# Respreading the start of a fused cross-attention and factor-sum kernel: row statistics and bias on VectorE, the second group's attention beside ten products

## The chip, the cores and the metric

The kernel runs on one core of a Trainium2 chip. That core has five engines, each of which works through its own instruction queue in order: TensorE (PE, with its weight loads, PEld, beside it), VectorE (DVE), ScalarE (ACT), GpSimd (POOL) and SyncE (SP), which here only issues DMAs. [...]The metric is device time in microseconds (us) of one execution; lower is better.

## The reference

`x` is 8 batches of 1024 rows of 1024 float32 values; each batch has 64 memory rows with a mask, and there are eight 1024x1024 factors. Cut to what matters:

```python
def _layernorm(x, eps=1e-05):
    m = mean(x); v = var(x)
    return (x - m) / sqrt(v + eps)

def xattn(h, mem, mask):
    scores = einsum('bsd,bmd->bsm', h, mem) / sqrt(D)
    scores = where(mask, scores, -1e30)
    out = einsum('bsm,bmd->bsd', softmax(scores), mem)
    return where(any(mask), out, 0)

def ffn(h, factors, bias):
    return einsum('btd,rde->bte', h, factors) / sqrt(8) + bias

x = x + xattn(layernorm(x), ctx, mask)
x = x + ffn(layernorm(x), factors, bias)
```

The sum over `r` can be done first: with W = the sum of the eight factors, the second line is one 1024x1024 product per row. W has to be summed once, from 32 MB of factors, before the products can be finished.

## The kernel before, in words

**Tiling.** The 8192 rows are 16 groups (`NG`) of 512 rows, two groups to a batch. A group is four tiles of 128 rows, `x_g_t`, kept in a pool `xpool` of 12 buffers of 512 KB, from which the centred memory `memc` of a batch is also drawn. Another pool, `big`, has nine buffers of 1 MB: factor slices `f`, blocks `xb` of x, transposed x (`xT`), normalized rows `h`, their re-laid copy `hb` and the transposed rows `hT` all come from it. A tile whose buffer is still in use makes its first writer wait.

**Products.** The row product is done by a Winograd scheme: for each half group q (two row tiles) seven products (`UNITS`, u = 0 to 6) of 4 matmuls each, which the trace counts as 8, from left operands that `combine_rows` makes on VectorE and right operands that `combine_factors` makes from the quadrants of W. `product(g, q, u)` issues the matmuls into a PSUM bank, and `give(g, q, u)` adds the bank to the rows on VectorE. A group has 14 products.

**First part: four factor steps.** Each of four steps (`step` 0 to 3) sums two of W's eight chunks of rows. In round s = 0 to 3 of a step, SP loads two 1 MB factor slices, `f` (factor s) and `fp` (factor 4+s); TensorE adds `fp` into four PSUM banks by products with the identity (`sum_on_pe`, L423), VectorE adds `f` into SBUF (L535, from round 1 on), and then `beside(step, s)` issues a piece of attention work. At the end of a step VectorE adds the PSUM banks to the SBUF sums (L540) and combines (L429 to L433). The next step's L423 matmuls need the banks that L540 reads.

**Attention of a group.** Row statistics (`row_sums` and `row_squares` on ScalarE, then a power on GpSimd giving `rs`), transposes of x, `scores` (L205), `scores_back` (L221), `softmax` (L230 to L242; its first step needs `rs`), `weights_back` (L252 to L258), `read_out` (L268) and `residual` (L279) per half group; then `norm_stats` (VectorE, and four small GpSimd operations, L292 to L296), `normalize` (ScalarE, L308), and either `transpose_h_pe` (group 0) or `relayout` (16 DMAs of 64 KB, L327) followed by `transpose_rows` (VectorE, L334). `add_bias` adds the bias to the rows (GpSimd, L320). For a new batch, `centre_memory` (L109 to L112) makes `memc` on ScalarE with one small GpSimd step (L111), and `transpose_memory` (L120) transposes it on TensorE.

**Order.** All engines issue in the order in which the program is written, so the order of the calls in `beside` and in the loop over groups is the order in every queue. The attention of groups 0 and 1 and four products of group 0 (two of each half, `unit`) are in `beside`; the ten products of group 0 that are left are the first pass (g = 0) of the loop over groups. Passes g = 1 to 15 do 14 products each with the attention of group g+1, and the loads and transposes for g+2, beside them. In the first pass `store(0, 0)` is issued on SP at k = 7, `centre_memory(1)` at k = 9 and `transpose_memory(1)` at k = 11 (k counts 0 to 13 and includes the four products done earlier).

Of the kernel before, what the change touches and what calls it, by code (L numbers as in the profile page):

```python
# [20 lines left out]
def kernel(  # L21
# [81 lines left out]
    def centre_memory(b: int):  # L103


        m = st["mem", b]
        mc = xpool.tile([P, D], F32, tag="x", name=f"memc_{b}")
        msum = small.tile([P, 1], F32, tag="msum", name=f"msum_{b}")
        nc.scalar.activation(mc[:M], m[:M], AF.Copy, accum_out=msum[:M])  # L109
        mneg = small.tile([P, 1], F32, tag="mneg", name=f"mneg_{b}")  # L110
        nc.gpsimd.tensor_scalar_mul(mneg[:M], msum[:M], -1.0 / D)  # L111
        nc.scalar.activation(mc[:M], m[:M], AF.Identity, bias=mneg[:M])  # L112
        st["memc", b] = mc

    def transpose_memory(b: int):

        mc = st.pop(("memc", b))
        ps = bank(f"memTp_{b}")
        for c in range(NC):
            nc.tensor.transpose(ps[:, ts(c, M)], mc[:M, c::NC], ident[:M, :M])  # L120
        mT = work.tile([P, NC, M], F32, tag="memT", name=f"memT_{b}")
        nc.scalar.copy(mT.rearrange("p c m -> p (c m)"), ps)
        st["memT", b] = mT
# [19 lines left out]
    def row_sums(g: int):  # L143
        s1 = small.tile([P, 4], F32, tag="s1", name=f"sum_{g}")
        junk = work.tile([P, D], F32, tag="junk", name=f"junk_{g}")
        for t in range(4):
            nc.scalar.activation(junk, st["x", g, t], AF.Copy, accum_out=s1[:, t : t + 1])  # L147
        nmean = small.tile([P, 4], F32, tag="nmean", name=f"nmean_{g}")
        nc.gpsimd.tensor_scalar_mul(nmean, s1, -1.0 / D)  # L149
        st["nmean", g] = nmean  # L150

    def row_squares(g: int):
# [10 lines left out]
        nc.gpsimd.tensor_tensor(rs, rs, neghalf, ALU.pow)  # L163
        st["rs", g] = rs

    def transpose_blocks(g: int, h: int):
        xb = st["xb", g, h]
        xT = big_tile([P, NC, 8 * Q], f"xT_{g}_{h}")
        nc.vector.transpose(  # L169
            xT.rearrange("p c (t j) -> p t c j", j=Q), xb.rearrange("p t (i c) -> p t c i", i=Q)  # L170
        )
        st["xb", g, h] = xT
# [10 lines left out]
    def transpose_x_pe(g: int, h: int):  # L183
        xT = big_tile([P, NC, 2 * P], f"xT_{g}_{h}")
        flat = xT.rearrange("p c t -> p (c t)")
        rows = [st["x", g, 2 * h + t] for t in range(2)]
        transpose_rows_pe(rows, 2, 2, lambda c0: flat[:, c0 * 2 * P : (c0 + 2) * 2 * P])
        st["xb", g, h] = xT
# [84 lines left out]
    def residual(g: int, q: int):  # L273
        rden = st["rden", g]
        for n in range(2):
            for h in range(2):
                xt = st["x", g, 2 * h + q][:, ts(n, H)]
                k = 2 * q + h
                nc.vector.scalar_tensor_tensor(  # L279
                    xt, st.pop(("ro", g, q, n, h)), rden[:, k : k + 1], xt, ALU.mult, ALU.add  # L280
                )
# [32 lines left out]
            )  # L314
        st["h", g, q] = h2

    def add_bias(g: int, q: int):
        for h in range(2):
            xt = st["x", g, 2 * h + q]
            nc.gpsimd.tensor_add(xt, xt, bias_bc)  # L320

    def relayout(g: int, q: int, eng):
        h2 = st.pop(("h", g, q))
# [120 lines left out]
    nc.vector.tensor_reduce(valid, maskf, AX.X, ALU.max)  # L444
    nc.vector.tensor_scalar(maskf, maskf, NEG, -NEG, ALU.mult, ALU.add)

    done = set()

    def unit(g: int, q: int, u: int):
        product(g, q, u)  # L450
        give(g, q, u)
        done.add((g, q, u))

    def beside(i: int, s: int):
        if (i, s) == (0, -1):
            centre_memory(0)
            transpose_memory(0)
            transpose_x_pe(0, 0)
            transpose_x_pe(0, 1)
            scores(0)  # L460
            row_sums(0)
            row_squares(0)
        if (i, s) == (0, 0):
            scores_back(0)
        if (i, s) == (0, 1):
            softmax(0)
            nc.scalar.dma_start(bias_bc, bias.partition_broadcast(P))
        if (i, s) == (0, 2):
            weights_back(0)
            read_out(0, 0)  # L470
            residual(0, 0)
        if (i, s) == (0, 3):
            norm_stats(0, 0)
            read_out(0, 1)
            residual(0, 1)
        if (i, s) == (1, 0):
            normalize(0, 0, False)
            norm_stats(0, 1)
            transpose_h_pe(0, 0)
        if (i, s) == (1, 1):  # L480
            add_bias(0, 0)
            normalize(0, 1, False)
            transpose_h_pe(0, 1)
        if (i, s) == (1, 2):
            combine_rows(0, 0)
            load_rows(1, nc.sync)
        if (i, s) == (1, 3):
            add_bias(0, 1)
        if (i, s) == (2, 0):
            unit(0, 0, 0)  # L490
            unit(0, 0, 1)
        if (i, s) == (2, 1):
            combine_rows(0, 1, (1,))
            transpose_x_pe(1, 0)
        if (i, s) == (2, 2):
            transpose_x_pe(1, 1)
            row_sums(1)
        if (i, s) == (2, 3):
            scores(1)
            row_squares(1)  # L500
        if (i, s) == (3, 0):
            scores_back(1)
            softmax(1)
        if (i, s) == (3, 1):
            weights_back(1)
            read_out(1, 0)
            residual(1, 0)
        if (i, s) == (3, 2):
            norm_stats(1, 0)
            read_out(1, 1)  # L510
            normalize(1, 0)
            relayout(1, 0, nc.scalar)
            residual(1, 1)
        if (i, s) == (3, 3):
            norm_stats(1, 1)
            normalize(1, 1)
            relayout(1, 1, nc.scalar)
            unit(0, 1, 0)
            unit(0, 1, 1)

    for step in range(NS):
# [20 lines left out]
    ring[:] = COMMON  # L542


    for g in range(NG):
        n, m = g + 1, g + 2
        more, most = n < NG, m < NG
        attend = more and n > 1
        fresh = most and m % GPB == 0
        if g > 0:  # L550
            store(g - 1, 1, nc.sync)
        if most:
            load_blocks(m, nc.sync)
            load_rows(m, nc.sync)
        for k in range(14):
            q, u = divmod(k, 7)
            if (g, q, u) not in done:
                product(g, q, u)
            if k == 0:
                if g > 0:  # L560
                    combine_rows(g, 0, (4, 3))
                if attend:
                    scores(n)
            if k == 1:
                if g > 0:
                    transpose_rows(g, 1)
                if attend:
                    scores_back(n)
            if k == 2 and attend:
                softmax(n)  # L570
            if k == 3:
                if attend:
                    weights_back(n)
                if g > 0:
                    combine_rows(g, 1, (1, 2))
            if k == 4:
                if attend:
                    read_out(n, 0)
                if most:
                    row_sums(m)  # L580
                combine_rows(g, 1, (4, 3) if g > 0 else (2, 4, 3))
                if g > 0:
                    add_bias(g, 1)
            if k == 5 and attend:
                residual(n, 0)
            if k == 6 and attend:
                norm_stats(n, 0)
                read_out(n, 1)
            if k == 7:
                if fresh:  # L590
                    load_memory(m // GPB, nc.sync)
                store(g, 0, nc.sync)
                if attend:
                    normalize(n, 0)
                    relayout(n, 0, nc.sync)
                    residual(n, 1)
            if k == 8 and more:
                if attend:
                    norm_stats(n, 1)
                add_bias(n, 0)  # L600
                if attend:
                    normalize(n, 1)
                    relayout(n, 1, nc.sync)
            if k == 9 and most:
                transpose_blocks(m, 0)
                if fresh:
                    centre_memory(m // GPB)
                row_squares(m)
            if k == 10 and most:
                transpose_blocks(m, 1)  # L610
            if k == 11 and fresh:
                transpose_memory(m // GPB)
            if k == 12 and more:
                transpose_rows(n, 0)
            if k == 13 and more:
                combine_rows(n, 0, (1, 2))
            if (g, q, u) not in done:
                give(g, q, u)
    store(NG - 1, 1, nc.sync)


# [26 lines left out]
```

## Time and profile before

| What | Time or value |
|---|---|
| median of 3 runs | 1045.17 us (1044.82 to 1047.14) |
| the profiled execution, its own time | 1046.43 us |
| its span, first to last instruction | 1044.6 us |
| PE busy | 1000.0 us (96%) |
| DVE / ACT / POOL busy | 659.8 / 359.3 / 224.6 us |
| mean granted TensorE clock | 0.984 |
| 13.6 to 192.5 us (factor steps and ten products): PE busy, clock | 152.18 of 178.90 us, 0.90 |
| 192.5 to 1044.6 us (groups 1 to 15): PE busy, clock | 847.79 of 852.10 us, 1.00 |

How to read it: the first matmul is at 13.62 us, and the first product of group 1 starts at 192.48 us. From there to the end TensorE is almost always busy at full clock. The stretch between those two points is where the trace has idle time of TensorE and a clock below 1. A timeline line gives the start, the time from the first to the last of the merged instructions, the engine, the line of the program, the operation with output and inputs, the count, and in brackets how long the engine had been idle and who ended that.

### The profile page before, as it was taken

Reading aid. Unit: us, or ns where it says so; the run is one execution under the profiler, and the core shown is the slowest. Engines: PE = TensorE matmul, PEld = TensorE weight load, DVE = VectorE, ACT = ScalarE, POOL = GpSimd, SP = SyncE. Lnnn points to the kernel's source line nnn. Section 1 sums busy time; section 2 is a strip of 40 time slices with the busy share of each in tenths; the row PEclk is TensorE's granted clock in tenths of the full one; section 3 lists DMA queues with packets and bytes.
Section 4 is the critical chain, followed back from the end, with each engine's and each line's share of the span. In section 5 each row is a group of like instructions: output and inputs, shape, how many; then the busy total and the mean of one; then the engine's idle time right before and its main releaser. Section 6 shows DMA issues by size and latency. Waiting matters only on the chain.

```text
span 1044.6 us, 8939 instructions
## 1 busy us (share of the span) xinstructions
PE 1000.0 (96%) x2912; PEld 447.8 (43%) x2912; DVE 659.8 (63%) x875; ACT 359.3 (34%) x537; POOL 224.6 (22%) x255
## 2 busy tenths in 40 slices
PE   4789887999999999999999999999999999999998
PEld 3245333444444444444444444444444444444443
DVE  1595666476675858585766767585857676685541
ACT  4322332233442526241434335252524234340300
POOL 0150001031222213040412222130404022240400
PEclk9889899999999999999999999999999999999999
DMA  9877637636556474828474556638482746540321
GB/s 322 323 289 317 239 83 218 153 107 157 161 151 165 99 197 121 221 81 192 135 167 133 139 143 170 172 105 215 110 212 89 169 156 154 158 108 33 91 81 50
DMA packets 93519, 166.89 MB, mean 160 GB/s; under 512 B 12320, under 2 KB 71840, under 8 KB 89376
## 3 DMA queue, kind: packets, MB, share of 16 engines
q1 hardware_dynamic: 90464, 163.10, 54.0%
q10 hardware_dynamic: 3008, 3.21, 1.3%
q8 instruction: 23, 0.38, 0.2%
q14 instruction: 24, 0.20, 0.1%
HBM read 101.25 MB, written 33.55 MB: 129 GB/s over the span
## 4 chain that ended last, share of the span: by engine, by line
PE 88%; issue 4%; DVE 3%; DMA 2%; ACT 2%; POOL 1%; SPq 0%; ACTq 0%; DVEq 0%; POOLq 0%
PE yu L385 40%; PE yv L385 20%; PE yz L385 11%; PE ro L268 6%; PE scT L205 6%; PE sum L423 2%; DMA f<-in_L_ffn_factors_dram 1%; ACT junk L158 1%; DMA mem<-in_ctx_dram 1%; PE memTp L120 1%; DVE x L279 1%; PE tp L180 1%; DVE st L289 1%; DVE b L535 1%; POOL x L320 0%
## 5 line engine op out<-in xcount | busy, mean ns | idle before, releaser
L385 PE MATMUL yu<-t,hT 128*128 128x512 f32 x512 | 230.2, 592 | 0.0
L308 ACT ACTIVATE h<-x,nb,rstd 128x1024 f32<-128x1024 f32 x64 | 137.4, 2196 | 233.4 <-POOL nb L296 156.3
L398 DVE SCALAR_TENSOR_TENSOR x<-yu,x 128x512 f32<-128x512 f32 x128 | 88.0, 688 | 160.9 <-PE yu L385 160.9
L320 POOL TENSOR_TENSOR x<-x,bias_bc 128x1024 f32<-128x1024 f32 x64 | 152.3, 2402 | 0.0
L385 PEld LDWEIGHTS yu<-t,hT 128*128 128x128 f32 x512 | 96.2, 190 | 115.8 <-issue 115.8
L385 PE MATMUL yu<-t,s 128*128 128x512 f32 x256 | 116.1, 596 | 4.0 <-DVE t L432 4.0
L385 PE MATMUL yz<-b,hT 128*128 128x512 f32 x256 | 119.4, 610 | 0.0
L385 PE MATMUL yu<-b,hT 128*128 128x512 f32 x256 | 116.5, 598 | 0.0
L385 PE MATMUL yv<-t,s 128*128 128x512 f32 x256 | 116.5, 598 | 0.0
L385 PE MATMUL yv<-b,s 128*128 128x512 f32 x256 | 116.1, 596 | 0.0
L169 DVE STREAM_TRANSPOSE xT<-xb 128x2048 f32<-128x2048 f32 x28 | 109.8, 3922 | 0.0
L398 DVE SCALAR_TENSOR_TENSOR x<-yv,x 128x512 f32<-128x512 f32 x64 | 43.7, 683 | 97.9 <-PE yv L385 93.2
L149 POOL TENSOR_SCALAR nmean<-sum 128x4 f32<-128x4 f32 x16 | 4.1, 257 | 437.1 <-ACT junk L147 437.1
L279 DVE SCALAR_TENSOR_TENSOR x<-ro,rden,x 128x512 f32<-128x512 f32 x128 | 87.4, 744 | 16.7 <-PE ro L268 16.7
L289 DVE BATCH_NORM_STATS2 st<-x 128x6 f32<-128x512 f32 x128 | 80.2, 668 | 0.0
L385 PEld LDWEIGHTS yv<-b,s 128*128 128x128 f32 x256 | 49.2, 192 | 62.3 <-issue 62.3
L147 ACT ACTIVATE junk<-x 128x1024 f32<-128x1024 f32 x64 | 67.5, 1055 | 24.0 <-DMA x<-in_x_dram 21.5
L385 PEld LDWEIGHTS yu<-b,hT 128*128 128x128 f32 x256 | 47.5, 190 | 65.1 <-issue 65.1
L385 PEld LDWEIGHTS yz<-b,hT 128*128 128x128 f32 x256 | 47.7, 193 | 64.3 <-issue 52.5
L158 ACT ACTIVATE junk<-x,nmean 128x1024 f32<-128x1024 f32 x64 | 73.3, 1145 | 1.9 <-POOL nmean L149 0.4
L385 PEld LDWEIGHTS yv<-t,s 128*128 128x128 f32 x256 | 47.5, 190 | 59.9 <-issue 57.2
L385 PEld LDWEIGHTS yu<-t,s 128*128 128x128 f32 x256 | 47.5, 190 | 58.9 <-issue 54.0
(67 smaller groups left out, 796.4 us busy)
## 6 DMA issues: line engine op xcount, KB each, us to landing
x<-in_x_dram SPq DMA_DIRECT2D x64, 512.0 KB, 10.2
f<-in_L_ffn_factors_dram SPq DMA_DIRECT2D x32, 1024.0 KB, 11.1
out_dram<-x SPq DMA_DIRECT2D x64, 512.0 KB, 2.9
xb<-in_x_dram SPq DMA_DIRECT2D x112, 256.0 KB, 7.1
hb<-h SPq DMA_DIRECT2D x448, 64.0 KB, 2.0
mem<-in_ctx_dram SPq DMA_DIRECT2D x14, 256.0 KB, 3.8
hb<-h ACTq DMA_DIRECT2D x32, 64.0 KB, 2.1
mem<-in_ctx_dram ACTq DMA_DIRECT2D x2, 256.0 KB, 10.4
```

The lines of the kernel that those rows point to most:

```text
L147: nc.scalar.activation(junk, st["x", g, t], AF.Copy, accum_out=s1[:, t : t + 1])
L158: nc.scalar.activation(junk, st["x", g, t], AF.Square, bias=nmean[:, t : t + 1], accum_out=ss[:, t : t + 1])
L169: nc.vector.transpose(xT.rearrange("p c (t j) -> p t c j", j=Q), xb.rearrange("p t (i c) -> p t c i", i=Q))
L205: nc.tensor.matmul(ps[ts(h, M), : 2 * P], mT[:, c, :], st["xb", g, h][:, c, :], start=(c == 0), stop=(c == NC - 1),)
L268: nc.tensor.matmul(ps, eT[ts(h, M), q, :], m[ts(h, M), ts(n, H)], start=True, stop=True)
L279: nc.vector.scalar_tensor_tensor(xt, st.pop(("ro", g, q, n, h)), rden[:, k : k + 1], xt, ALU.mult, ALU.add)
L289: nc.vector.bn_stats(stats[:, n, :], xt[:, ts(n, H)])
L308: nc.scalar.activation(dst, src, AF.Identity, bias=nb[:, h : h + 1], scale=rstd[:, h : h + 1],)
L320: nc.gpsimd.tensor_add(xt, xt, bias_bc)
L385: nc.tensor.matmul(ps, lhs[:, c, :], wq[rhs][:, c, :], start=(first and c == 0), stop=(c == KH - 1), skip_group_check=True,)
L398: nc.vector.scalar_tensor_tensor(xt, st["y", g, q, key], ISR, xt, ALU.mult, ALU.add)
L423: nc.tensor.matmul(banks[c, n], ident, f[:, c, ts(n, H)], start=first, stop=last)
```

## The change

The change touches the order of work up to group 1, and nothing after it.

- Group 0's row statistics: `row_sums(0)` and `row_squares(0)` on ScalarE are replaced by `row_stats(0)` on VectorE (8 `bn_stats`, 4 `bn_aggr`, two GpSimd operations), issued first of all, and `transpose_x_pe(0, 0)` is put ahead of `centre_memory(0)`.
- Group 0's attention is spread over more rounds (steps 0 to 2), and its `add_bias` is done by VectorE.
- Group 1's attention up to `softmax(1)` stays in the factor steps, one piece a round; the rest (`weights_back(1)` to `transpose_rows(1, 0)`) moves beside the ten products, which get a loop of their own (k = 0 to 9). Its relayouts are issued by SP instead of ScalarE.
- In that loop `load_memory(1)` is at k = 4, `store(0, 0)` and `centre_memory(1)` at k = 6 behind `relayout(1, 1)`, `transpose_memory(1)` at k = 8 and `add_bias(1, 0)` at k = 9.
- The loop over groups starts at g = 1 with the same order as before; its conditions become shorter.

```diff
+    def row_stats(g: int):
+        mv = small.tile([P, 4, 2], F32, tag="mvx", name=f"mvx_{g}")
+        for t in range(4):
+            stats = small.tile([P, 2, 6], F32, tag="stats", name=f"stx_{g}_{t}")
+            for n in range(2):
+                nc.vector.bn_stats(stats[:, n, :], st["x", g, t][:, ts(n, H)])
+            nc.vector.bn_aggr(mv[:, t, :], stats)
+        rs = small.tile([P, 4], F32, tag="rs", name=f"rs_{g}")
+        nc.gpsimd.tensor_scalar(rs, mv[:, :, 1], EPS, float(D), ALU.add, ALU.mult)
+        nc.gpsimd.tensor_tensor(rs, rs, neghalf, ALU.pow)
+        st["rs", g] = rs
...
-    def add_bias(g: int, q: int):
+    def add_bias(g: int, q: int, eng=nc.gpsimd):
...
-            nc.gpsimd.tensor_add(xt, xt, bias_bc)
+            eng.tensor_add(xt, xt, bias_bc)
...
         if (i, s) == (0, -1):
+            row_stats(0)
+            transpose_x_pe(0, 0)
             centre_memory(0)
+            transpose_x_pe(0, 1)
             transpose_memory(0)
-            transpose_x_pe(0, 0)
-            transpose_x_pe(0, 1)
             scores(0)
-            row_sums(0)
-            row_squares(0)
...
         if (i, s) == (0, 2):
             weights_back(0)
+        if (i, s) == (0, 3):
             read_out(0, 0)
             residual(0, 0)
-        if (i, s) == (0, 3):
+        if (i, s) == (1, 0):
             norm_stats(0, 0)
             read_out(0, 1)
+        if (i, s) == (1, 1):
+            normalize(0, 0, False)
             residual(0, 1)
-        if (i, s) == (1, 0):
-            normalize(0, 0, False)
+        if (i, s) == (1, 2):
             norm_stats(0, 1)
             transpose_h_pe(0, 0)
-        if (i, s) == (1, 1):
-            add_bias(0, 0)
-            normalize(0, 1, False)
-            transpose_h_pe(0, 1)
-        if (i, s) == (1, 2):
-            combine_rows(0, 0)
             load_rows(1, nc.sync)
         if (i, s) == (1, 3):
-            add_bias(0, 1)
+            normalize(0, 1, False)
+            add_bias(0, 0, nc.vector)
         if (i, s) == (2, 0):
+            transpose_h_pe(0, 1)
+            combine_rows(0, 0)
             unit(0, 0, 0)
+        if (i, s) == (2, 1):
             unit(0, 0, 1)
-        if (i, s) == (2, 1):
+            add_bias(0, 1, nc.vector)
+        if (i, s) == (2, 2):
             combine_rows(0, 1, (1,))
             transpose_x_pe(1, 0)
-        if (i, s) == (2, 2):
-            transpose_x_pe(1, 1)
             row_sums(1)
         if (i, s) == (2, 3):
-            scores(1)
+            transpose_x_pe(1, 1)
             row_squares(1)
         if (i, s) == (3, 0):
+            scores(1)
+        if (i, s) == (3, 1):
             scores_back(1)
+        if (i, s) == (3, 2):
             softmax(1)
-        if (i, s) == (3, 1):
-            weights_back(1)
-            read_out(1, 0)
-            residual(1, 0)
-        if (i, s) == (3, 2):
-            norm_stats(1, 0)
-            read_out(1, 1)
-            normalize(1, 0)
-            relayout(1, 0, nc.scalar)
-            residual(1, 1)
+            unit(0, 1, 0)
         if (i, s) == (3, 3):
-            norm_stats(1, 1)
-            normalize(1, 1)
-            relayout(1, 1, nc.scalar)
-            unit(0, 1, 0)
             unit(0, 1, 1)
...
+    load_blocks(2, nc.sync)
+    load_rows(2, nc.sync)
+    for k, (q, u) in enumerate((q, u) for q in range(2) for u in range(2, 7)):
+        product(0, q, u)
+        if k == 0:
+            weights_back(1)
+        if k == 1:
+            read_out(1, 0)
+            combine_rows(0, 1, (2,))
+        if k == 2:
+            residual(1, 0)
+            row_sums(2)
+        if k == 3:
+            norm_stats(1, 0)
+            read_out(1, 1)
+        if k == 4:
+            combine_rows(0, 1, (4, 3))
+            normalize(1, 0)
+            relayout(1, 0, nc.sync)
+            load_memory(2 // GPB, nc.sync)
+        if k == 5:
+            residual(1, 1)
+        if k == 6:
+            norm_stats(1, 1)
+            normalize(1, 1)
+            relayout(1, 1, nc.sync)
+            store(0, 0, nc.sync)
+            centre_memory(2 // GPB)
+            row_squares(2)
+        if k == 7:
+            transpose_blocks(2, 0)
+        if k == 8:
+            transpose_memory(2 // GPB)
+            transpose_blocks(2, 1)
+        if k == 9:
+            transpose_rows(1, 0)
+            add_bias(1, 0)
+        give(0, q, u)
+    combine_rows(1, 0, (1, 2))
...
-    for g in range(NG):
+    for g in range(1, NG):
```

More of the change, by code (lines that the diff above doesn't have):

```diff
@@ L445 @@
     nc.vector.tensor_scalar(maskf, maskf, NEG, -NEG, ALU.mult, ALU.add)
-    done = set()
     def unit(g: int, q: int, u: int):
@@ L451, in unit @@
         give(g, q, u)
-        done.add((g, q, u))
     def beside(i: int, s: int):
         if (i, s) == (0, -1):
+            row_stats(0)
+            transpose_x_pe(0, 0)
             centre_memory(0)
+            transpose_x_pe(0, 1)
             transpose_memory(0)
-            transpose_x_pe(0, 0)
-            transpose_x_pe(0, 1)
             scores(0)
-            row_sums(0)
-            row_squares(0)
         if (i, s) == (0, 0):
@@ L542 @@
     ring[:] = COMMON
-    for g in range(NG):
+    load_blocks(2, nc.sync)
[38 more added lines that the diff above has]
+    for g in range(1, NG):
         n, m = g + 1, g + 2
         more, most = n < NG, m < NG
-        attend = more and n > 1
         fresh = most and m % GPB == 0
-        if g > 0:
-            store(g - 1, 1, nc.sync)
+        store(g - 1, 1, nc.sync)
         if most:
@@ L556 @@
             q, u = divmod(k, 7)
-            if (g, q, u) not in done:
-                product(g, q, u)
+            product(g, q, u)
             if k == 0:
-                if g > 0:
-                    combine_rows(g, 0, (4, 3))
-                if attend:
+                combine_rows(g, 0, (4, 3))
+                if more:
                     scores(n)
             if k == 1:
-                if g > 0:
-                    transpose_rows(g, 1)
-                if attend:
+                transpose_rows(g, 1)
+                if more:
                     scores_back(n)
-            if k == 2 and attend:
+            if k == 2 and more:
                 softmax(n)
             if k == 3:
-                if attend:
+                if more:
                     weights_back(n)
-                if g > 0:
-                    combine_rows(g, 1, (1, 2))
+                combine_rows(g, 1, (1, 2))
             if k == 4:
-                if attend:
+                if more:
                     read_out(n, 0)
@@ L580 @@
                     row_sums(m)
[L581 to L584, printed above, removed]
+                combine_rows(g, 1, (4, 3))
+                add_bias(g, 1)
+            if k == 5 and more:
                 residual(n, 0)
-            if k == 6 and attend:
+            if k == 6 and more:
                 norm_stats(n, 0)
@@ L592 @@
                 store(g, 0, nc.sync)
-                if attend:
+                if more:
                     normalize(n, 0)
@@ L597 @@
             if k == 8 and more:
-                if attend:
-                    norm_stats(n, 1)
+                norm_stats(n, 1)
                 add_bias(n, 0)
-                if attend:
-                    normalize(n, 1)
-                    relayout(n, 1, nc.sync)
+                normalize(n, 1)
+                relayout(n, 1, nc.sync)
             if k == 9 and most:
@@ L616 @@
                 combine_rows(n, 0, (1, 2))
-            if (g, q, u) not in done:
-                give(g, q, u)
+            give(g, q, u)
     store(NG - 1, 1, nc.sync)
```

## The prediction, made before the result was known

> **What bounds the kernel now.** I read the page's slices first, then the windows, then the timelines of TensorE, VectorE and SP up to 260 us, and the waits of SP. TensorE (PE) is the bound: of the span it is busy 96%, and the low digits stand in the first seven slices (26.1 us each) and at the very end.
>
> ```profile
> span 1044.6 us, 8939 instructions
> PE   4789887999999999999999999999999999999998
> PEclk9889899999999999999999999999999999999999
> 192.50:1044.60 852.10, 847.79 (x2457) 375.80 (x2455) 553.19 (x749) 293.43 (x428) 194.65 (x215) 1.00 0.53 140
> ```
>
> From 192.5 us, group 1's first product, PE is busy 847.79 of 852.10 us at full clock, and the change leaves that order alone. So the question is when group 1 starts: every us earlier is a us of the total. In the stretch before it PE waits at these places (timeline; the bracket is the idle time and what ended it):
>
> ```profile
> 35.07 0.42 DVE L230 TENSOR_TENSOR sm<-sc,rs 128x256 f32<-128x256 f32 x1 [11.07 <-POOL rs L163]
> 37.27 0.33 PE L256 MATMUL eTp<-ident,e 128*128 128x128 f32 x1 [3.41 <-ACT e L242]
> 52.54 6.37 PE L423 MATMUL sum<-f,ident 128*128 128x512 f32 x8 [3.45 <-DVE b L540]
> 66.29 2.73 DVE L366 TENSOR_TENSOR s<-hT,s 128x512 f32<-128x512 f32 x1
> 74.23 8.83 PE L423 MATMUL sum<-f,ident 128*128 128x512 f32 x16 [4.22 <-DMA f<-in_L_ffn_factors_dram]
> 143.14 1.88 PE L385 MATMUL yu<-t,s 128*128 128x512 f32 x4
> 149.00 2.71 PE L385 MATMUL yu<-t,s 128*128 128x512 f32 x4 [3.98 <-DVE t L432]
> 182.35 1.14 PE L120 MATMUL memTp<-ident,memc 64*128 64x64 f32 x8 [5.64 <-ACT memc L112]
> 183.42 5.79 PE L385 MATMUL yz<-b,hT 128*128 128x512 f32 x8
> 189.05 3.60 PE L385 MATMUL yu<-t,hT 128*128 128x512 f32 x8
> ```
>
> The reader is to see three things. Softmax stood 11.07 us on VectorE for `rs`, and group 0's factor adds stood behind it. Eight matmuls of 512 take 3.60 us normally (3.43 from start to start), but 6.37 or 5.79 after a wait. And the last wait of the stretch is for `memc`. What `memc` hangs on is in the next lines: SP's store of group 0's first rows, and, for the changed order, the relayout DMAs and `normalize`.
>
> ```profile
> 167.32 0.49 SPq L403 DMA_DIRECT2D out_dram<-x  x1
> 177.57 1.06 ACT L109 ACTIVATE memc<-mem 64x1024 f32<-64x1024 f32 x1 [1.57 <-DMA out_dram<-x]
> 136.55 10.45 ACTq L327 DMA_DIRECT2D hb<-h  x16
> 147.10 4.40 ACT L308 ACTIVATE h<-x,nb,rstd 128x1024 f32<-128x1024 f32 x2 [10.58 <-DVE b L540]
> 229.39 21.09 SPq L327 DMA_DIRECT2D hb<-h  x32
> SPq L131 <- DMA hb<-h: 40.7, 6, 25.2
> out_dram<-x SPq DMA_DIRECT2D x64, 512.0 KB, 2.9
> ```
>
> `memc` takes a buffer of `xpool`; with three groups of rows in it all 12 are held, and ScalarE waited for a store to free one. A relayout's 16 DMAs take 10.45 us of the issuing queue on ACT, and half of 21.09 on SP.
>
> **What the Trainium skill says.** "TensorE: Matmul & The Clock Gate", What's actually happening: after an idle window of about 3.4 us the PE clock is halved, until a busy window has passed. The trace agrees: the windows view has 0.50 for 40 to 44 and 52 to 56 us, after the idles above. "SBUF — State Buffer", SBUF: two separate sides: GpSimd and a VectorE operation with two SBUF inputs exclude each other. Agrees: L366 took 2.73 us while GpSimd's L320 ran, where 0.69 is usual (249.88 and 267.64 us). "DMA: Bandwidth & Descriptors", Issuing engines are not separate DMA queues: another issuing engine saves only the issue time on the sequencer. Agrees for the relayout (0.65 us per DMA on either).
>
> **Part 1: up to the end of the fourth product (143.14 us before: that is `unit(0,1,1)`'s end).** I walk the new order with the old durations.
>
> Start. x's loads are issued at 0.7 to 2.1 us and land 5.8 to 12.1 us later, so by 14.2. `row_stats` is 8 x 0.61 + 4 x 0.13 = 5.4 us of VectorE, mostly under the landings: done 15.7, `rs` 17.1 (GpSimd 0.24 + 1.04). The ScalarE work that goes (4 x 1.18 + 4 x 1.27 = 9.8 us) was the 11.07 us wait. A price: `centre_memory(0)`'s GpSimd step is now queued behind the two `rs` operations, so `memc` is at 18.5 instead of 13.6; the copies of the second transposes queue behind it on ScalarE (to 20.9), then `memT` 21.5, and scores end at 25.1 where they ended at 23.1: +2.
>
> Step 0: three PE sums 3.44 each with the two transposes of 0.25 to 35.8, eT 36.2, sum to 39.7, read-out to 40.7, residual 4 x 0.70 to 42.8. VectorE's softmax comes at 28.9, as soon as scores are back, so its adds are never late. L540 starts 42.8, not 51.8, and PE waits 2.7 us for it to 43.4 (52.54 before): 9 us won.
>
> Step 1: the sums are 13.8, read-out 1.0, transposes of h 2.2: PE would be at 60.4; the factors bind just as much. By 20 us 5.9 MB had moved; up to this step's last slice 22 MB must, and the queue moves 422 GB/s when it has work: 20 + 16.1/0.422 = 58 us, 60 with the bias. Last sum ends 63.5, L540 (VectorE's bias, 2 x 1.2, ends 64.1 ahead of it) frees the first bank at 64.7.
>
> Steps 2 and 3 are PE's: 8 sums 27.6, transposes 2.3 + 4.7, scores 3.6, four products 4 x 3.43 = 13.7, score transposes 0.25, which is 52.2: 64.7 + 52.2 = 116.9. Of the nine buffers hT takes two, and xT two from round (2,2) on; the last slices are then issued at 99.7, as scores(1) frees xT, and land at 104.5 and 107 (4.8 alone, 2.5 behind another) where PE needs the last at 110. Group 0's bias on VectorE is 4.9 us and frees the adds from GpSimd's lock (about 8 us lost in 63.5 to 75 before); VectorE per step is 11 to 20 us, under PE's. The waits that remain (2.7 at 40.7, some 2 at 58 and 64) can halve the clock for a window of 3.4 us each, 1.7 us lost; the first falls under the factors. I add 2.5: **119.5**, against 143.14: -23.6.
>
> **Part 2: the ten products.** Before: 143.14 to 192.48 = 49.3, of which 34.3 products, 1.1 memory transposes, 3.98 + 5.64 idle, the rest clock. After, from 119.5: the chain give, L540, t3, t2 stays after the last unit (k = 0 ends at +8.4, 127.9, as 143.14 to 151.5), eT 0.4, k = 1 4.4 (half clock, as before), read-out 1.0, k = 2 and 3 6.9, read-out 1.4 (its fourth bank is the z product's, freed by `give`), so k = 6 starts at 148.9 and k = 8 ends at 159.2. Beside that, from k = 6: give 0.8, `norm_stats(1,1)` 2.75 to 152.5, GpSimd 1.7 (138.70 to 140.40 before), `normalize` 4.4 to 158.7, sixteen relayout DMAs on SP 10.5 to 169.2, and only then `store(0,0)`, which lands 2.9 us after issue: 172.3. `memc` needs that buffer: 12 are held by groups 0, 1 and 2. ScalarE and GpSimd 2.7: 175.0. `transpose_memory` sits in PE's queue after k = 8, and k = 9 and group 1 behind it: **PE waits from 159.2 to 175.0, 15.8 us** where it waited 5.64. VectorE's new work a round is at most 2.75 (residual or statistics) + 0.6 under a product's 3.43, so hidden; only the two block transposes (3.9 + 0.6, at k = 7 and 8) run over, by 2 us in all, and the stall covers that (without it they cost up to 2). Then 1.1 + 3.43, and 2.7 for the half clock (5.79 - 3.43 = 2.4 before): group 1 starts at 182.2. Behind it GpSimd's bias on group 1 now runs at about 181 to 186, beside `combine_rows(1,0)`: at 2.75 instead of 0.69 apiece VectorE is some 4 us late, and a give that PE needs about 1.3 us: 183.5.
>
> What is taken away has its worth too: ScalarE's 32 relayout issues (20.8 us) and the loads of group 2 that stood behind them (25.2 us the longest) go, which is why `row_sums(2)` no longer ends that stretch; it is the store that is late next.
>
> **The sum.** 192.48 - 183.5 = 9.0 us. The profiled execution took 1046.43 us, so 1037.4 for its like; the median of the runs is 1.3 lower: **1036**. Unknown costs: part 1 ends 116 to 123 (no further clock loss, or two more windows and 3 us of late factors); the stall is 14 (less if part 1 hides some) to 18; the bias behind it 0 to 2. That gives 1031 to 1042.
>
> **Rivals.** (1) The stall is not there, `memc` gets a buffer or a store lands sooner: for it, only one read of one wait says that the buffer is the store's; against it, 12 row tiles are counted. Then part 2 is 41 us, 1016 to 1020. Chance 0.08. (2) The store lands as late as the one before did (167.32 to 177.5, 10.1 us, with 3 MB queued): stall 7 more, 1043. Against it: the queue is idle at 169. 0.08. (3) Part 1 comes out nearer its PE work, 112: 1029. 0.08. (4) The slower one: the factor queue starves in steps 1 to 3. It stood idle for some 27 us before (44 to 48, 52 to 60, 88 to 95, 115 on) since each slice waits for a buffer; if the new order holds buffers as long (h, hT, xT each in turn, one slice late by 4.8 us a time), part 1 ends at 136, wins 7 and pays about 13 in part 2: 1051. It decides from an end of part 1 past 132.5 us. 0.20, of which a small part lies near zero. The likeliest, as worked out: 0.56.
>
> **How the numbers follow.** About 0.2% (2 us) is what a measurement here can tell from none. Faster: 0.56 + 0.08 + 0.08 + 0.08 = 0.80; within 0.2%: 0.03 and slower 0.17, both from rival 4. The range 1028 to 1046 leaves rival 1 and most of rival 4 out.
>
> **What would show it.** Step by step: softmax's L230 near 29 us with no long wait; L540 of step 0 near 43; the first left product near 119 with the same 4 us wait for t2; one PE wait of about 16 us for `memc` ahead of L120, behind SP's relayout and store; group 1's first product near 183. No such wait would show part 2 wrong; a last factor landing past 115 would show part 1 wrong.

## The result, and the profile after

The changed kernel takes 1038.08 us (median of 4 runs, 1037.1 to 1038.24), the kernel before 1045.29 us beside it. The ratio is 0.9926, 95% interval 0.9909 to 0.9943: 7 to 8 us faster. The profiled execution took 1037.97 us with a span of 1035.7 us, 8.9 us shorter than that of the kernel before.

The page's first lines of the changed kernel answer to those shown of the kernel before. The windows below them give, for each stretch, its length, the busy time of PE, PEld, DVE, ACT and POOL with the instruction counts, then the granted clock, the DMA share and GB/s.

```profile
span 1035.7 us, 8927 instructions
...
PE   5999894999999999999999999999999999999998
...
PEclk9999996999999999999999999999999999999999
```

```profile
20.00:72.00 52.00, 46.81 (x156) 22.14 (x156) 37.80 (x52) 11.37 (x23) 7.32 (x8) 0.93 1.01 420
...
13.60:183.50 169.90, 141.39 (x440) 68.09 (x440) 101.45 (x131) 52.22 (x88) 16.35 (x27) 0.92 0.71 260
183.50:1035.70 852.20, 847.81 (x2457) 375.79 (x2455) 557.88 (x751) 293.77 (x428) 199.62 (x217) 1.00 0.53 140
```

Group 1's first product starts at 183.51 us where it started at 192.48. From there to the end it is 852.2 us, as before (852.1): the whole difference lies in front of it. Slices 2, 3 and 6 of PE, 7, 8 and 8 before, are 9 now, and slice 7 (155 to 181 us) has fallen from 7 to 4, together with a clock of 0.6. The first window shows the DMA queue moving 420 GB/s from 20 to 72 us; in the kernel before it moved 305 GB/s in the same stretch:

```profile
20.00:72.00 52.00, 42.10 (x138) 19.45 (x134) 36.36 (x44) 20.86 (x39) 16.20 (x15) 0.87 0.76 305
```

The new low digit is one wait. TensorE, ScalarE and SP in the timeline of the changed kernel (start, duration, engine, line, operation, count, and in brackets the idle time before and who ended it):

```profile
120.29 1.88 PE L398 MATMUL yu<-t,s 128*128 128x512 f32 x4
126.15 2.79 PE L398 MATMUL yu<-t,s 128*128 128x512 f32 x4 [3.98 <-DVE t L445]
177.12 1.14 PE L120 MATMUL memTp<-ident,memc 64*128 64x64 f32 x8 [15.38 <-ACT memc L112]
178.19 5.48 PE L398 MATMUL yu<-t,hT 128*128 128x512 f32 x8
183.51 3.60 PE L398 MATMUL yu<-b,hT 128*128 128x512 f32 x8
```

```profile
161.15 10.26 SPq L340 DMA_DIRECT2D hb<-h  x16
174.44 1.06 ACT L109 ACTIVATE memc<-mem 64x1024 f32<-64x1024 f32 x1 [13.32 <-DMA out_dram<-x]
```

The four early products end at 120.29 us (143.14 before), so 22.9 us were won. The ten left products then take 63.2 us (49.3 before), so 13.9 us were given back. Of these, 9.7 are the longer wait for `memc`, 15.38 us instead of 5.64; the rest is in the main the two read-outs that have moved here (1.9 us of TensorE each). While TensorE stands for `memc`, ScalarE stands for a store (13.32 us), and that store was issued only when SP had got through the 16 relayout DMAs. The chain of waits of the changed kernel has the same order, in pieces of start, time and what:

```profile
156.73 4.41 ACT h L321 x2
...
170.82 0.59 SPq L340
171.41 0.05 issue
171.51 2.85 DMA out_dram<-x
174.40 0.04 issue
174.44 1.16 ACT memc L109 x2
```

### The profile page after: what moved, and what is told of

The parts are those of the page before. It is cut to its first block, busy times and chain, and to the rows that moved or that the text cites. A ratio compares the mean times of both kernels' runs of the same rounds, so it can differ in the third digit from the quotient of the medians.

```text
span 1035.7 us, 8927 instructions
## 1 busy us (share of the span) xinstructions
PE 993.5 (96%) x2912; PEld 447.3 (43%) x2912; DVE 664.2 (64%) x891; ACT 349.9 (34%) x521; POOL 216.7 (21%) x250
## 4 chain that ended last, share of the span: by engine, by line
PE 91%; DVE 3%; ACT 1%; DMA 1%; SPq 1%; issue 1%; POOL 0%; ACTq 0%
PE yu L398 43%; PE yv L398 21%; PE yz L398 11%; PE scT L218 6%; PE ro L281 6%; PE sum L436 4%; DMA x<-in_x_dram 1%; SPq L340 1%; PE memTp L120 1%; DVE st L302 1%; DVE x L292 1%; DVE b L538 0%; ACT h L321 0%; PE tp L193 0%; PE eTp L269 0%
## 5 line engine op out<-in xcount | busy, mean ns | idle before, releaser
L333 POOL TENSOR_TENSOR x<-x,bias_bc 128x1024 f32<-128x1024 f32 x60 | 141.7, 2383 | 0.0
L398 PE MATMUL yz<-b,hT 128*128 128x512 f32 x256 | 117.2, 600 | 0.0
L398 PEld LDWEIGHTS yu<-b,hT 128*128 128x128 f32 x256 | 47.4, 190 | 64.7 <-issue 64.7
L347 DVE STREAM_TRANSPOSE hT<-hb 128x1024 f32<-128x1024 f32 x60 | 70.8, 1219 | 0.1
L158 ACT ACTIVATE junk<-x,nmean 128x1024 f32<-128x1024 f32 x60 | 68.7, 1146 | 1.5
## 6 DMA issues: line engine op xcount, KB each, us to landing
mem<-in_ctx_dram ACTq DMA_DIRECT2D x2, 256.0 KB, 10.4
```

What stands on the lines that cost most here:

```text
L158: nc.scalar.activation(junk, st["x", g, t], AF.Square, bias=nmean[:, t : t + 1], accum_out=ss[:, t : t + 1])
L333: eng.tensor_add(xt, xt, bias_bc)
L347: nc.vector.transpose(hT[:, h].rearrange("p c (t j) -> p t c j", j=Q), hb[:, h].rearrange("p t (c i) -> p t c i", i=Q),)
L398: nc.tensor.matmul(ps, lhs[:, c, :], wq[rhs][:, c, :], start=(first and c == 0), stop=(c == KH - 1), skip_group_check=True,)
```

## The experiments

My theory: the gain in front is TensorE's waits filled by a wider spread and by work moved out of the factor steps, and the larger part of what is lost again is lost because `memc` needs a row buffer which only `store(0, 0)` frees, and that store is queued on SP behind a relayout. Each ratio below is to the kernel before, measured beside the run; the changed kernel's is 0.9926. A point in time is read from one execution. The changed kernel and runs 1 to 3 are the same up to the end of the early products, and reach it at 119.80 to 120.93 us; so a difference of about 1 us there tells nothing.

**1. The store ahead of the relayout.**

```diff
         if k == 6:
+            store(0, 0, nc.sync)
             norm_stats(1, 1)
             normalize(1, 1)
             relayout(1, 1, nc.sync)
-            store(0, 0, nc.sync)
```

> The changed kernel with store(0,0) issued on SP ahead of the second relayout of group 1 instead of behind it; nothing else. Theory (memc waits for a row buffer that only this store frees): the store leaves SP at about 161 us, right after the memory load, and lands at 164; memc ready at about 166.7; TensorE's wait ahead of the memory transposes falls from 15.4 to about 5 us, so the time falls by 10 to 11 us, to about 1027.5. Rival (the wait is for the relayouts themselves or for ScalarE's normalize, and the store is only the last event seen): no change, 1037 to 1039.

Measured: 1030.65 us, ratio 0.9846 (0.9827 to 0.9865). The wait fell to 6.19 us:

```profile
165.17 1.06 ACT L109 ACTIVATE memc<-mem 64x1024 f32<-64x1024 f32 x1 [4.11 <-DMA out_dram<-x]
167.85 1.14 PE L120 MATMUL memTp<-ident,memc 64*128 64x64 f32 x8 [6.19 <-ACT memc L112]
```

The store left SP at 160.87 us and landed after 4.3 us, not 3, with the memory load just ahead of it. That is the 1.2 us by which the wait is longer than expected. This trace is of the fastest of the four executions (1028.06 us), close to the 1027.5 expected; why the median is some 2.6 us above it was not looked into. The rival is out: the relayout is no shorter (11.34 us on SP, 10.26 before) and the wait is.

**2. The buffer taken away from the wait, the store left where it is.**

```diff
-        mc = xpool.tile([P, D], F32, tag="x", name=f"memc_{b}")
+        if b == 1:
+            mc = big_tile([P, D], f"memc_{b}")
+        else:
+            mc = xpool.tile([P, D], F32, tag="x", name=f"memc_{b}")
```

> The changed kernel with the store left where it is, but the centred memory of batch 1 drawn from the pool of large buffers, so that it needs no row buffer. Theory: memc then waits for the memory load alone, which SP issues at 160 us behind the first relayout, and for ScalarE, which is busy to 161 us: ready at about 166.5, the wait is about 5 us, time about 1027.5. Rival (the store's place in SP's queue, not the buffer, decides): no change.

Measured: 1027.16 us, ratio 0.9818 (0.9801 to 0.9836). ScalarE's wait has another name now, the memory load, and TensorE's is 3.90 us:

```profile
162.47 1.06 ACT L112 ACTIVATE memc<-mem 64x1024 f32<-64x1024 f32 x1 [1.83 <-DMA mem<-in_ctx_dram]
165.16 1.14 PE L123 MATMUL memTp<-ident,memc 64*128 64x64 f32 x8 [3.90 <-ACT memc L115]
```

By their ratios these two runs are some 8 and 11 us faster than the changed kernel. The two edits have nothing in common but the buffer that the store frees: one has it freed sooner, the other does without it. So the buffer and the store's place in SP's queue together make the wait.

**3. The wait taken away in full.**

```diff
         if k == 4:
             combine_rows(0, 1, (4, 3))
+            load_memory(2 // GPB, nc.sync)
             normalize(1, 0)
             relayout(1, 0, nc.sync)
-            load_memory(2 // GPB, nc.sync)
         if k == 5:
+            store(0, 0, nc.scalar)
+            centre_memory(2 // GPB)
             residual(1, 1)
...
-            store(0, 0, nc.sync)
-            centre_memory(2 // GPB)
             row_squares(2)
```

> The changed kernel with the memory load ahead of the first relayout on SP, store(0,0) on ScalarE's queue at k = 5 and centre_memory at k = 5. Theory: memc is ready at about 155 us, seven us before TensorE comes to the memory transposes (161.6), so the wait and the half clock behind it go: group 1 starts at about 166 to 167 instead of 183.5, time 1021 to 1023. What is late next is transpose_rows(1,0) on VectorE behind the block transposes (done at 166.6), at most 1 us. Rival (TensorE then meets another late engine, the second relayout or GpSimd's bias): 1026 to 1032.

Measured: 1021.21 us, ratio 0.9759 (0.974 to 0.9778). TensorE comes to the memory transposes at 163.26 us and does not stop, and group 1 starts at 167.82 us:

```profile
159.73 3.60 PE L398 MATMUL yz<-b,hT 128*128 128x512 f32 x8
163.26 1.09 PE L120 MATMUL memTp<-ident,memc 64*128 64x64 f32 x8
164.28 3.70 PE L398 MATMUL yu<-t,hT 128*128 128x512 f32 x8
167.82 3.60 PE L398 MATMUL yu<-b,hT 128*128 128x512 f32 x8
```

No other engine takes the place of the wait; the two block transposes, which the prediction thought could cost up to 2 us without it, cost nothing. This version has the changed kernel's gain ahead of the ten products without what it gives back.

**4. Group 0's statistics back on ScalarE, the rest as changed.**

```diff
-            row_stats(0)
             transpose_x_pe(0, 0)
             centre_memory(0)
             transpose_x_pe(0, 1)
             transpose_memory(0)
             scores(0)
+            row_sums(0)
+            row_squares(0)
```

> The changed kernel with group 0's row statistics back on ScalarE behind its scores, the new spread of the attention kept. Theory (the statistics were the gate of step 0 and TensorE's queue, not the factor loads, bounds step 1): softmax at about 38.5 instead of 30.7 us, step 0's bank sums 3 to 5 us later, and this passes through to the end with a half-clock window: 1041 to 1044. Rival (step 1 waits for factor slices anyway, as the prediction's 60 us had it): at most 1 us slower, 1038 to 1039.

Measured: 1039.95 us, ratio 0.994 (0.9925 to 0.9954), which the intervals do not tell apart from the changed kernel. The early products end at 121.49 us, only 1.2 us later than there. The size was wrong, and so was the rival's reason: no sum of step 1 waits for a factor slice in this trace. Without `row_stats` at the head of the queues, scores end at 21.95 us, where the changed kernel's end at 26.62, so this version starts its sums 4.7 us sooner and loses that at softmax. Softmax's first operation, here and then in the changed kernel:

```profile
33.95 0.42 DVE L243 TENSOR_TENSOR sm<-sc,rs 128x256 f32<-128x256 f32 x1 [9.70 <-POOL rs L163]
30.65 0.43 DVE L243 TENSOR_TENSOR sm<-sc,rs 128x256 f32<-128x256 f32 x1 [6.52 <-PE sc L234]
```

In the place where the change has it, `row_stats` costs almost what it saves.

**5. Group 0's bias back on GpSimd.**

```diff
-            add_bias(0, 0, nc.vector)
+            add_bias(0, 0)
...
-            add_bias(0, 1, nc.vector)
+            add_bias(0, 1)
```

> The changed kernel with group 0's two bias additions on GpSimd again, in the same rounds. Theory (in the new order VectorE has slack in steps 1 and 2, TensorE's queue bounds, so it doesn't matter which engine adds): within 1.5 us of the changed kernel, 1036.5 to 1039.5; the VectorE operations with two SBUF inputs beside it take some 2.7 us instead of 0.7. Rival (GpSimd's lock on VectorE was a real part of the loss before, as the prediction charged with about 8 us): 4 to 8 us slower.

Measured: 1037.38 us, ratio 0.9914 (0.9901 to 0.9928), the changed kernel's value within the intervals. What the prediction calls GpSimd's lock, the slowing of VectorE's operations with two SBUF inputs beside a GpSimd operation, is there, and TensorE doesn't feel it:

```profile
65.11 11.19 POOL L333 TENSOR_TENSOR x<-x,bias_bc 128x1024 f32<-128x1024 f32 x4
71.36 2.73 DVE L377 TENSOR_TENSOR s<-s,hT 128x512 f32<-128x512 f32 x1
76.77 0.68 DVE L381 TENSOR_TENSOR hT<-hT 128x512 f32<-128x512 f32 x1
```

While GpSimd adds the bias, the same kind of VectorE operation takes 2.73 us, and 0.68 us as soon as it has ended. The early products end at 119.63 us all the same.

**6. The statistics behind the memory's centring.**

```diff
-            row_stats(0)
             transpose_x_pe(0, 0)
             centre_memory(0)
+            row_stats(0)
```

> The changed kernel with row_stats(0) issued behind centre_memory(0), so that the memory's small GpSimd step is no longer queued behind the two for rs. Theory (that queueing costs the start 4.7 us: scores ended at 26.6 here and at 21.95 without it): scores end at about 22, step 0's bank sums come 4.5 us earlier, and 2.5 to 4.5 us of it reach the end, the rest going to the factor loads, which run at full rate up to 72 us: 1033.5 to 1035.5. Rival (the factor stream alone sets the end of step 1): under 1 us gained, 1037 to 1038.

Measured: 1038.72 us, ratio 0.9918 (0.9905 to 0.9931): not told apart from the changed kernel. The scores end at 23.68 us, not 22, because their 32 matmuls took 5.47 us where the theory counted on 3.67. Step 1's first sum starts at 42.59 us, 2.9 sooner than 45.53, and then TensorE waits for factor slices, which it doesn't in the changed kernel:

```profile
60.39 3.70 PE L436 MATMUL sum<-f,ident 128*128 128x512 f32 x8 [1.74 <-DMA f<-in_L_ffn_factors_dram]
65.45 3.67 PE L436 MATMUL sum<-f,ident 128*128 128x512 f32 x8 [1.36 <-DMA f<-in_L_ffn_factors_dram]
```

The early products end at 118.89 us, 1.4 sooner, in this trace, which is of the fastest of the five executions (1035.68 us). Runs 10 and 11 below have the same start: their scores take 3.67 us and end at 23.05 and 21.78 us, TensorE then waits for factor slices from step 0 on, and the early products end at 119.57 and 120.69 us. So the queueing does cost the scores some 3 to 5 us, but the theory had its worth at the end too large; the rival is nearer. Up to about 66 us the changed kernel runs close to the pace of the factor loads, and a faster start has little left to win.

**7 and 8. Parts of the change alone, put into the kernel before.** Run 7 replaces the statistics only; run 8 adds the bias on VectorE.

```diff
         if (i, s) == (0, -1):
             centre_memory(0)
+            row_stats(0)
...
-            row_sums(0)
-            row_squares(0)
```

```diff
-            add_bias(0, 0)
+            add_bias(0, 0, nc.vector)
...
-            add_bias(0, 1)
+            add_bias(0, 1, nc.vector)
```

> The kernel before with one part of the change alone: group 0's statistics by row_stats on VectorE, issued behind centre_memory(0). Theory (the statistics gated step 0 only; residual and norm_stats of both halves stay in its last rounds): step 0's bank sums start at about 47 instead of 51.8, and 4 to 6 us reach the end: 1039 to 1042 where the kernel before is 1045.3. Rival (this part is nearly the whole of what the change gained ahead of the ten products, 22.9 us): below 1030. Other rival (the factor wait at 74 us swallows it): 1044 to 1046.

> The kernel before with two parts of the change: row_stats as in the run above, and group 0's bias on VectorE. Theory: VectorE's operations at 63 to 75 us take their 0.7 us again, which saves up to 8 us of it and costs 4.7, so 0 to 3 us less than the run above: 1037 to 1041; the rest of the change's early gain is the spread of the steps and the attention moved beside the ten products. Rival (the lock was on the path in full): 8 us less than the run above.

Measured: 1041.67 us, ratio 0.9951 (0.9937 to 0.9964), and 1042.11 us, ratio 0.996 (0.9947 to 0.9972). The statistics alone give some 5 us; the bias adds nothing to them. In run 7 the early products end at 138.30 us, in run 8 at 141.12 us. The wait for a factor at step 1's last sum, 4.22 us before, is still 4.11 us in run 7 and 4.02 us in run 8, where GpSimd adds no bias beside it. In run 7:

```profile
69.53 8.83 PE L436 MATMUL sum<-f,ident 128*128 128x512 f32 x16 [4.11 <-DMA f<-in_L_ffn_factors_dram]
```

**9. The spread without the move.** The kernel before with the changed kernel's statistics, bias and rounds up to (2, 1); group 1's attention stays in the factor steps, and the pass over group 0 is the one of before. The core of it, against the changed kernel:

```diff
         if (i, s) == (2, 1):
             unit(0, 0, 1)
             add_bias(0, 1, nc.vector)
+            combine_rows(0, 1, (1,))
+            transpose_x_pe(1, 0)
         if (i, s) == (2, 2):
-            combine_rows(0, 1, (1,))
-            transpose_x_pe(1, 0)
+            transpose_x_pe(1, 1)
             row_sums(1)
...
+        if (i, s) == (3, 1):
+            weights_back(1)
+            read_out(1, 0)
+            residual(1, 0)
...
```

> The kernel before with the statistics, the VectorE bias and the wider spread of group 0's attention (the changed kernel's rounds up to (2, 1)), but with group 1's attention where it was, in steps 2 and 3, and the pass over group 0 as before. Theory: the last early product ends about 12.7 us later than in the changed kernel (4.4 us of TensorE's work for group 1, 4.5 of waits, 3.4 of half clock stay in step 3), near 133, and the ten products then cost about 49 as before, with the 5.6 us wait for memc: group 1 starts near 182.5 and the time is 1034 to 1038. So the move beside the ten products gains early what the memc wait takes. Rival (the spread alone does little, and the move makes the net gain): 1040 to 1043.

Measured: 1036.15 us, ratio 0.9902 (0.9888 to 0.9916). The early products end at 132.79 us, group 1 starts at 182.44. The move out of the factor steps is worth 12.5 us at the end of the early products (132.79 against 120.29), and nothing at the end: the changed kernel, with the move, starts group 1 at 183.51, and the intervals do not tell the two apart. What is left in step 3 of this version is what the move took out:

```profile
107.24 0.33 PE L269 MATMUL eTp<-ident,e 128*128 128x128 f32 x1 [1.78 <-ACT e L255]
110.77 2.73 PE L281 MATMUL ro<-mem,eT 64*128 64x512 f32 x4 [0.84 <-DVE x L292]
113.43 5.35 PE L436 MATMUL sum<-f,ident 128*128 128x512 f32 x8
138.65 3.78 PE L398 MATMUL yu<-t,s 128*128 128x512 f32 x4 [3.98 <-DVE t L445]
```

Short waits for softmax and residual, and behind them four matmuls (counted as 8) that take 5.35 us instead of 3.60; the clock granted from 113 to 117 us was 0.53.

**10 and 11. A version that beats both.** Run 10 puts the edits of 3 and 6 together. Run 11 also takes the products of each half in another order, so that the first does not need t2, the last but one of the four results b22, t3, t2 and t4 that VectorE makes one after another:

```diff
-    for k, (q, u) in enumerate((q, u) for q in range(2) for u in range(2, 7)):
+    for k, (q, u) in enumerate((q, u) for q in range(2) for u in (3, 2, 4, 5, 6)):
```

> The version without the wait for memc (memory load ahead of the relayout, store on ScalarE, centre_memory at k = 5), with row_stats(0) behind centre_memory(0) as well. Theory: the two add up, the second by what it gave alone, some 1 to 1.5 us: about 0.9745 of the kernel before, 1019 to 1021. Rival (the start is covered by the factor loads again): no difference from the first alone, 0.976.

> The same version with the products of each half in the order u = 3, 2, 4, 5, 6, so that the first of the ten needs b22 and not t2, which VectorE finishes 2.5 us later. Theory: TensorE's wait of 4.0 us behind the last early product falls to about 1.6 and half a clock window with it: 2.4 to 4 us less than the version above, 1016 to 1018. Rival (VectorE's chain of four additions sets the second product instead, the wait only moves): under 1 us.

Measured: 1020.33 us, ratio 0.9751 (0.9737 to 0.9765), and 1017.11 us, ratio 0.9718 (0.9704 to 0.9732). Run 10 is not told apart from run 3; its rival was right. Run 11 is some 3 us faster than run 10. In its trace the 3.98 us wait is 0.86 us:

```profile
123.43 1.98 PE L398 MATMUL yv<-b,s 128*128 128x512 f32 x4 [0.86 <-DVE b L538]
```

Group 1 starts at 162.87 us there, 29.6 us sooner than in the kernel before.

## Why the prediction was right, point by point

The forecast was 1036 us with a gain of 9.0; the spans differ by 8.9, the medians by 7.2. The mechanism it named on each side is the one the runs showed. That the start of group 1 was hit to 0.01 us (183.5) is luck, as the terms below show. The forecast also took the median to lie 1.3 us below the profiled execution, as in the kernel before; here it lies 0.1 above it (1038.08 and 1037.97), and this is most of the 2.1 us by which the time was missed.

| Step of the prediction | predicted | measured |
|---|---|---|
| `rs` ready | 17.1 | 17.4 |
| scores end | 25.1 | 26.6 |
| softmax's first operation | 28.9 | 30.65 |
| L540 of step 0 (L538 after) | 42.8 | 44.80 |
| step 2's first sum | 64.7 | 66.49 |
| end of the early products | 119.5 | 120.29 |
| k = 6 starts | 148.9 | 151.28 |
| second relayout on SP, end | 169.2 | 171.41 |
| TensorE's wait for `memc` | 15.8 | 15.38 |
| product behind it, beyond 3.43 | 2.7 | 2.05 |
| group 1 starts | 182.2 | 183.51 |
| bias of group 1 behind it | 1.3 | 0 |

**The start.** That the memory's GpSimd step would queue behind the two operations for `rs` was seen, and priced at 2 us. It is 3.5, because the scores ran at a lower clock, 0.68 from 21.3 to 26.6 us: 32 matmuls took 5.36 us where they take 3.67. The short waits of TensorE ahead of them (1.60 and 0.83 us) are a likely reason, which no run tried by itself; all six traces with this start have it, with 5.01 to 6.23 us. Runs 6, 10 and 11 show that little or nothing of the loss reaches the end, since the factor loads are next.

**Read-outs.** A `read_out` was priced at 1.0 us. The trace has 1.99 for its four matmuls; I had read the count of 8 as two read-outs. This term is about a us short three times, and half a us in the last, which was priced at 1.4: twice ahead of the early products' end and twice in the ten products. Step 2's first sum came 1.8 us late and the end of the early products only 0.8: of the 2.5 us that I had added for half clock, steps 2 and 3 used about 1.6 (53.8 us, where their work was priced at 52.2). So the end of part 1 is close in part because an allowance was too large.

**GpSimd's lock.** The sentence that VectorE's bias "frees the adds from GpSimd's lock (about 8 us lost ...)" named a true effect in the wrong place. The lock is real (2.73 against 0.68 us in run 5), but it was not on the path in either order: runs 5 and 8 moved the time by nothing that can be told, and in run 8 the wait for a factor stayed when the lock had gone. The sum didn't use it, as steps 2 and 3 were priced by TensorE's work alone.

**The bias behind the wait.** VectorE was slowed as predicted (2.01 and 2.73 us for L375 and L377 at 184 us), but no give was late enough for TensorE to notice: no idle from 183.5 us on. That 1.3 us and the 1.3 us by which group 1 started late cancel in the sum.

**Rivals.** The first (no wait) and the second (the store lands after 10 us) did not come; the store landed in 2.9. The third had part 1 end at 112; it ended at 120.29. The fourth, a starved factor queue, is the opposite of what happened: 420 GB/s from 20 to 72 us. Its reading of the kernel before was a little off at the end: the queue did not stay idle from 115 us on, but moved 272 and 252 GB/s from 116 to 120 and from 120 to 124 us. Run 7, with the old spread, keeps the wait for a factor, and the changed kernel, with the new one, has none; whether it is the later `h` and `xT` tiles that free the buffers sooner was argued from the order of the program and not tried by itself.

**Where the 22.9 us came from.** By the end of the early products: 143.14 before, 138.30 with the statistics (4.8, issued behind `centre_memory`), 141.12 with the bias too, 132.79 with the spread as well (and `row_stats` at the head), 120.29 with the move (12.5). So the statistics, the bias and the spread together are worth 10.4 us; how these divide is known only roughly, as the bias seems to take back 2.8 in one trace and changes no time. The parts were measured in this order only; in the changed order the statistics are worth 1.2 us (run 4), hardly more than two traces of one order differ. The prediction did not divide this gain and so said nothing wrong of it, but its reader would have given the statistics too much.

## What to carry to other kernels

When work is moved beside a busy stage, follow its DMAs through the queue that issues them: here the sixteen relayout DMAs went to SP in front of a store, and the buffer which that store frees was a third engine's, two queues away. A full pool turns a store into a producer, so stores that free buffers go ahead of transfers that nobody needs soon. And a gain early in a kernel is only a gain when the next stage's waits are counted again with the new start times.

## What was not expected of the hardware

A long wait of TensorE cost no more clock than a short one: the product behind 15.38 us of idle took 5.48 us, the one behind 5.64 us in the kernel before 5.79, and the one behind 3.90 us in run 2 took 5.92, all against 3.60. Nor is the price of a given wait fixed, and it does not take the 3.4 us of idle with which the prediction counted: the sum behind the 2.55 us wait at the start of step 1 took 5.25 us in the changed kernel (clock 0.54 from 45.5 to 49 us), 4.04 in runs 2 and 10 and 5.73 in run 11. For a batch of small DMAs the issue is the main cost here: 0.64 us of SP for each relayout DMA of 64 KB, 10.26 us for sixteen, while each lands about 2 us after its issue.
